# Six short attention tiles: exponentials transposed by TensorE in place of a split, a DMA and a join

## The chip, the cores and the metric

The kernel runs on one core of a Trainium2 chip, in one launch. The metric is the device time of one execution in microseconds (us); lower is better. Engines are named as in the profile: PE is TensorE's matmul, PEld its weight load, DVE is VectorE, ACT is ScalarE, POOL is GpSimd, and SP is the engine that issues most of the DMAs.

## The reference

The input x has 2 batches of 2048 rows of 512 numbers. All arithmetic is in f32.

```python
xn = layernorm(x)
# attention, causal, one head of width 512
x_norm = layernorm(xn) * gamma + beta
q, k, v = (x_norm @ qkv[:, i * 512 : (i + 1) * 512] for i in range(3))
scores = where(causal, q @ k.T / sqrt(512), -inf)
s = softmax(scores) @ v @ o_proj + xn
# mixture of 8 experts, the best two of each row
top, idx = top_k(xn @ gate_w.T + gate_b + bias, 2)
h = silu(xn @ w1[e].T + b1[e]);  y_e = h @ w2[e].T + b2[e]
g = silu(sum of y_e over the two experts, weighted by softmax(top))
return x + s * g
```

Softmax over the keys of a row means: the maximum of its scores, exponentials of the scores less the maximum, their sum as a divisor, and the product of the exponentials with v.

## The kernel before

Rows are taken in tiles of 128. There are 32 tiles, 16 to a batch. The program has three stages. In the first one the rows are normed and projected, and the experts' routing is worked out. In the second one the experts run. In the third one, which starts at about 595 us and is the one that matters here, attention runs and the outputs are put together. The order of instructions on every engine is the order in which the program writes them (a manual schedule), so an engine that waits holds up all that stands behind it.

The attention stage is a loop over steps s. Tiles are taken in the order of `seq`: the first batch from its last tile to its first, so that s = 15 is tile 0, then the second batch in the order 8, 9, 0, 1, 6, 7, 2, 3, 4, 5, 10 to 15. Tile t of a batch sees t + 1 blocks of 128 keys. `widths[s]` holds these keys cut into chunks of at most 512. In step s the program writes, in this order:

- `attended(s - 3)` (ScalarE line 1237, VectorE line 1240) and `emit(s - 4)` (two POOL operations, lines 1248 and 1249, and the output's DMA), for tiles outside the pairs named `FAST`.
- `fetch_inputs(s - 1)`: the DMA of the tile's input rows, on SP.
- `chunk_scores(s, j)` for each chunk (TensorE line 963; on VectorE the mask, line 968, and the maximum, line 969), and in between, on VectorE, `join_p(s - 1, j)` (line 1051).
- `end_scores(s)`: the negated maximum `nm` (VectorE line 981); `divisor(s - 1)`: `ri` (lines 1200 and 1201).
- `exponentials(s)`: for each chunk the exponential on ScalarE (line 1035, into `pr`), a POOL copy that puts the upper and lower 16-bit halves of the f32 numbers apart (line 1039, into `pu`), and a transposing DMA of the 16-bit halves (line 1044, SP, into `puT`).
- `fetch_parts`: DMAs of keys, values and queries for later steps, on SP.
- `values(s - 2)`: the product of the transposed exponentials with v (TensorE line 1069), for tiles outside `FAST`.
- in odd steps `gate(s - 3)` (four VectorE operations, lines 1227 and 1228, and a Silu on ScalarE, line 1232) and `gather_y(s - 1)` (four indirect DMAs on POOL, line 1216).

`join_p` puts the transposed halves together again into `turned[s]`, the tile `pT` that the product takes as stationary operand. A tile's exponentials so pass ScalarE, POOL, a DMA and VectorE, from step s to step s + 1, ahead of their product in step s + 2. `FAST` holds the pairs of tiles with s from 0 to 7 and from 26 to 31, whose product is made with seven half-size products in place of eight (line 1122); the tiles in between, s from 8 to 25, take `values`.

Buffers that matter: PSUM pool `ps_a` with five buffers of 128x512 f32, tag "a", for the scores; `ps_b` with three for the products; `pr` three, `pu` three, `puT` five, `pT` three. ScalarE switches between the table of the exponential and that of Silu with a table load, once each in two steps.

A transpose by TensorE is used elsewhere in the kernel: in `keys(0)` for the first four tiles of rows (line 286, copied from PSUM by ScalarE, line 287), and in `keep_scores` (line 322).

Of the kernel before, what the change touches and what calls it, by code (L numbers as in the profile page):

```python
# [10 lines left out]
F32 = mybir.dt.float32  # L11
# [9 lines left out]
P = 128  # L21
# [5 lines left out]
def gated_attention_moe(  # L27
# [27 lines left out]
    nc = tc.nc  # L55
# [3 lines left out]
    NT = B * S // P  # L59
    BT = 4  # L60
    TB = BT * P
    NB = NT // BT
    NBB = S // TB
# [31 lines left out]
    ident = const.tile([P, P], F32, name="ident")  # L95
# [856 lines left out]
    widths, scored, halves, turned, sums, gates, outs = {}, {}, {}, {}, {}, {}, {}  # L952
# [5 lines left out]
    def chunk_scores(s, j):  # L958
        b, t, first = place(s)
        w = widths[s][j]  # L960
        ps = ps_a.tile([P, TB], F32, name=f"ps_{s}_{j}", tag="a")
        for c in range(ND):
            nc.tensor.matmul(  # L963
                ps[:, :w], lhsT=aqs[seq[s] // 2][:, c, ts(t % 2, P)], rhs=aks[first + j][:, c, :w],
                start=(c == 0), stop=(c == ND - 1),
            )
        if first + j == b:
            nc.vector.tensor_tensor(ps[:, w - P : w], ps[:, w - P : w], keep, ALU.min)
        nc.vector.tensor_reduce(scored[s][0][:, j : j + 1], ps[:, :w], AX.X, ALU.max)  # L969
        scored[s][2].append(ps)  # L970

    def begin_scores(s):
        b, t, first = place(s)
        widths[s] = [TB] * (b - first) + [(t + 1) * P]
        mx = sm.tile([P, NBB], F32, name=f"mx_{s}", tag="mx")
        nm = sm.tile([P, 1], F32, name=f"nm_{s}", tag="nm")
        scored[s] = mx, nm, []
# [13 lines left out]
    ps_a = psum(att, name="ps_a", bufs=5)  # L991
# [13 lines left out]
    for i in range(NS):  # L1005
        experts_step(i)
        if i >= 8 and i % 2 == 0 and early:
            f, b, c = early.pop(0)
# [14 lines left out]
    tp = left(name="tp", bufs=3)  # L1023
# [4 lines left out]
    def exponentials(s):  # L1028

        _, nm, chunks = scored.pop(s)  # L1030
        rs = sm.tile([P, NBB], F32, name=f"rs_{s}", tag="rs")
        sums[s], halves[s] = rs, []
        for j, w in enumerate(widths[s]):
            pr = pp.tile([P, TB], F32, name=f"pr_{s}_{j}", tag="pr")
            nc.scalar.activation(  # L1035
                pr[:, :w], chunks[j][:, :w], AF.Exp, bias=nm, accum_out=rs[:, j : j + 1]
            )
            pu = php.tile([P, 2 * TB], U16, name=f"pu_{s}_{j}", tag="pu")
            nc.gpsimd.tensor_copy(  # L1039
                pu[:, : 2 * w].rearrange("p (h d) -> p h d", h=2),  # L1040
                pr[:, :w].bitcast(U16).rearrange("p (d h) -> p h d", h=2),
            )
            puT = php.tile([P, 2 * BT, P], U16, name=f"puT_{s}_{j}", tag="puT", bufs=5)
            nc.sync.dma_start_transpose(out=puT[:, : 2 * w // P, :], in_=pu[:, : 2 * w])
            halves[s].append(puT)

    def join_p(s, j):
        w = widths[s][j]
        if j == 0:
            turned[s] = tp.tile([P, NBB * TB], F32, name=f"pT_{s}", tag="pT")  # L1050
        nc.vector.tensor_copy(  # L1051
            turned[s][:, j * TB : j * TB + w].bitcast(U16).rearrange("p (i t h) -> p i t h", t=P, h=2),
            halves[s][j][:, : 2 * w // P, :].rearrange("p (h i) t -> p i t h", h=2),
        )

    def values(s):
        po = ps_b.tile([P, D], F32, name=f"po_{s}", tag="b")
        product(po, s, 0, place_keys(s), slice(0, D))
        outs[s] = po

    def place_keys(s):

        return place(s)[1] + 1 + (place(s)[0] - place(s)[2]) * BT

    def product(dst, s, k0, k1, cols, start=True):

        first = place(s)[2]
        for k in range(k0, k1):
            nc.tensor.matmul(  # L1069
                dst, lhsT=turned[s][:, ts(k, P)], rhs=avs[first + k // BT][:, k % BT, cols],  # L1070
                start=(start and k == k0), stop=(k == k1 - 1),
            )
# [9 lines left out]
    def combine_v(b, parts=(1, 2, 3, 4)):  # L1082

        n = 1 if b % NBB == NBB - 1 else 2
        v = avs[b].rearrange("p (i h) d -> p i h d", h=2)[:, :n]
        if 1 in parts:
            avts[b] = cp.tile(
                [P, n, 4, D // 2], F32, name=f"vT_{b}", tag=f"vT{n}", bufs=(1 if n == 1 else NBB - 1)
            )
        t1, t2, t3, t4 = (avts[b][:, :, i, :] for i in range(4))  # L1090
        b11, b12, b21, b22 = (v[:, :, h, c] for h in range(2) for c in (LO, HI))
        for i, dst, x1, x2 in (1, t1, b12, b11), (2, t2, b22, t1), (3, t3, b22, b12), (4, t4, b21, t2):
            if i in parts:
                nc.vector.tensor_tensor(dst, x1, x2, ALU.subtract)
# [109 lines left out]
    def fetch_inputs(s):  # L1204
        n = seq[s]
        xt = op.tile([P, D], F32, name=f"xo_{s}", tag="xo", bufs=5)
        nc.sync.dma_start(out=xt, in_=xb[:, n, :])
        gates[s] = [xt]
# [25 lines left out]
    def attended(s):  # L1234
        n = seq[s]
        o = outs[s] if s // 2 in FAST else op.tile([P, D], F32, name=f"o_{s}", tag="o", bufs=4)
        nc.scalar.activation(  # L1237
            o, outs[s], AF.Identity, scale=sums[s], bias=xshift[:, n : n + 1]
        )
        nc.vector.scalar_tensor_tensor(  # L1240
            o, gates[s][0], xscale[:, n : n + 1], o, ALU.mult, ALU.add
        )
        outs[s] = o

    def emit(s):
        xt, g = gates.pop(s)
        o = outs.pop(s)
        nc.gpsimd.tensor_tensor(o, o, g, ALU.mult)  # L1248
        nc.gpsimd.tensor_tensor(o, o, xt, ALU.add)  # L1249
        nc.sync.dma_start(out=ob[:, seq[s], :], in_=o)  # L1250
# [39 lines left out]
    def fetch_parts(s, most):  # L1290
        while parts_b and most and parts_b[0][0] <= s:
            _, f, b, c = parts_b.pop(0)
            f(b, c)
            most -= 1

    for s in range(NT + OUT + 2):
        fast = s // 2 - 1 in FAST
        if s < NT and s:
            begin_scores(s)
        if s == 1:  # L1300
            fetch_parts(s, 2 * ND)
        for k in range(NT):
            if k not in AHEAD:
                wait = 4 - k % 2 if k // 2 in FAST else 3
                if s == k + wait:
                    attended(k)
                if s == k + wait + 1:
                    emit(k)
        for k in range(NT):
            if s == (NT - 1 if k in AHEAD else k + 2 - k % 2 if k // 2 in FAST else k + 1):  # L1310
                fetch_inputs(k)
        joins = []
        if 0 <= s - 1 < NT - 1:
            joins = [(join_p, s - 1, j) for j in range(len(widths[s - 1]))]
        if s < NT:
            for j in range(len(widths[s])):
                if s:
                    chunk_scores(s, j)
                if joins:
                    f, *args = joins.pop(0)  # L1320
                    f(*args)
                if s == 2 and j:
                    for b in (0, 1) if j == 1 else (j,):
                        combine_v(b, (1,))
        for f, *args in joins:
            f(*args)
        if s < NT and s:
            end_scores(s)
        if fast and s % 2 == 0 and s < NT:
            combine_p(s - 2, range(NBB) if s == 2 else ())  # L1330
        if 0 <= s - 1 < NT:
            divisor(s - 1)
        if s < NT:
            exponentials(s)
            fetch_parts(s, 4 if s else 2 * ND)
            if s in combine:
                combine_v(combine[s])
        if fast and s % 2 == 0:
            values_first(s - 2)

            if s != NT - 2:
                values_next(s - 2)
        elif fast and s == NT - 1:
            values_next(s - 3)
            gate(s - 1)
            values_end(
                s - 3,
                [lambda j=j: join_p(s, j) for j in range(len(widths[s]))] + [lambda: combine_p(s - 1)],
            )
            for k in AHEAD:  # L1350
                make_ahead(k)
        elif fast:
            values_end(s - 3)
        elif 0 <= s - 2 < NT:
            values(s - 2)

        for k in range(0, NT - 2, 2):
            if s == (k + 2 if k + 2 in AHEAD else k + 3):
                gate(k)
        for k in range(0, NT, 2):  # L1360
            if s == (k if k in AHEAD else k + 1):
                gather_y(k)
                gather_y(k + 1)
# [45 lines left out]
```

## Time and profile before

| | us |
|---|---|
| median of 3 runs | 1072.64 (1067.35 to 1072.9) |
| the profiled execution | 1072.68 |
| its span | 1071.0 |
| TensorE busy | 1051.0 (98%) |
| VectorE busy | 598.7 (56%) |
| POOL busy | 422.1 (39%) |
| ScalarE busy | 310.6 (29%) |
| POOL split copies, line 1039, 80 of them | 85.1 |
| VectorE joins, line 1051, 80 of them | 61.0 |
| TensorE products of `values`, line 1069 | 82.9 |

The span is what the profile covers; 1.7 us of the execution's time lie around it. Busy times of the engines lie beside each other, so they don't add up to the span. A line of the profile names the engine, the line of the program, the operation, and output and inputs with buffer numbers left out. A matmul of f32 has two records on TensorE; a transpose of f32 has one. A bracket behind a line of a timeline tells how long the engine sat idle before it, and what is taken to have released it.

### The profile page before, as it was taken

How to read it: one execution, taken by the hardware profiler on the slowest of the kernel's cores; microseconds unless marked ns; L12 is line 12 of the kernel's file. 1: busy time of each engine (PE TensorE's matmuls, PEld its weight loads, DVE VectorE, ACT ScalarE, POOL GpSimd, SP SyncE). 2: the span in 40 equal slices, each digit the busy share in tenths (PEclk: the TensorE clock that was granted, in tenths of full speed). 3: DMA queues.
4: the chain of work that ended last, by engine and by line, in shares of the span. 5: the costliest groups of instructions: out<-in, count | busy, mean ns of one | idle time of the engine just before them, and what ended most of it. 6: DMA issues, size and time to landing. Idle time of an engine off the chain costs nothing.

```text
span 1071.0 us, 12108 instructions
## 1 busy us (share of the span) xinstructions
PE 1051.0 (98%) x3566; PEld 620.9 (58%) x3566; DVE 598.7 (56%) x1181; ACT 310.6 (29%) x659; POOL 422.1 (39%) x463
## 2 busy tenths in 40 slices
PE   8999999999999999999999999999999999999998
PEld 3687886444555555555545446776664444446677
DVE  5797884775333333333345338535555667675756
ACT  3212221211322232322355121312333343332330
POOL 2363240003433333333331023244557677574452
PEclk9999999999999999999999999999999999999999
DMA  8599989936999999999985186355668777763451
GB/s 305 170 282 280 276 257 335 351 123 176 225 222 234 226 227 227 232 226 224 214 187 131 42 224 145 91 122 156 154 176 231 219 201 207 202 171 91 108 141 40
DMA packets 303775, 210.11 MB, mean 196 GB/s; under 512 B 237784, under 2 KB 250840, under 8 KB 302688
## 3 DMA queue, kind: packets, MB, share of 16 engines
q1 hardware_dynamic: 284512, 146.91, 55.1%
q0 software_dynamic: 10560, 35.17, 13.1%
q10 hardware_dynamic: 8640, 27.27, 7.1%
q8 instruction: 30, 0.49, 0.2%
q14 instruction: 33, 0.27, 0.1%
HBM read 92.89 MB, written 60.03 MB: 143 GB/s over the span
## 4 chain that ended last, share of the span: by engine, by line
PE 65%; issue 13%; POOL 8%; DMA 5%; DVE 5%; SPq 2%; ACT 2%; ACTq 0%; POOLq 0%; DVEq 0%
PE ph L879 15%; PE py L918 15%; PE ps L963 13%; PE p L1122 10%; PE p L400 5%; PE pw L207 3%; DMA puT<-pu 2%; PE p L1069 2%; POOL yg L1216 2%; POOL pu L1039 1%; DMA zuT<-zu 1%; POOL o L1249 1%; POOL o L1248 1%; PE po L1069 1%; POOL zu L264 1%
## 5 line engine op out<-in xcount | busy, mean ns | idle before, releaser
L963 PE MATMUL ps<-k,q 128*128 128x512 f32 (+3 forms) x640 | 239.1, 529 | 0.0
L963 PEld LDWEIGHTS ps<-k,q 128*128 128x128 f32 x640 | 117.7, 190 | 122.0 <-issue 112.1
L918 PE MATMUL py<-w,ht 128*128 (+3 forms) x408 | 187.0, 594 | 0.0
L879 PE MATMUL ph<-w,xT 128*128 (+1 forms) x544 | 173.2, 460 | 0.7 <-POOL keep L1001 0.7
L1039 POOL COPY pu<-pr 128x1024 uint16<-128x1024 uint16 (+3 forms) x80 | 85.1, 1092 | 176.1 <-ACT pr L1035 158.1
L926 DVE COPY y<-py 128x512 f32<-128x512 f32 x68 | 46.9, 690 | 177.4 <-PE py L918 177.4
L879 PEld LDWEIGHTS ph<-w,xT 128*128 128x128 f32 (+1 forms) x544 | 97.5, 181 | 74.1 <-issue 35.2
L904 ACT ACTIVATE ht<-ht,b1sel 128x128 f32<-128x128 f32 (+3 forms) x237 | 73.1, 375 | 231.8 <-DVE ht L898 231.8
L889 POOL COPY hu<-h 128x704 uint16<-128x704 uint16 x68 | 52.3, 769 | 206.8 <-ACT h L887 145.5
L918 PEld LDWEIGHTS py<-w,ht 128*128 128x128 f32 (+3 forms) x408 | 73.5, 182 | 75.4 <-issue 37.4
L765 POOL DMA_INDIRECT xs<-zu_d,toki x68 | 69.1, 1017 | 75.7 <-DVE toki L642 64.3
L1035 ACT ACTIVATE pr<-ps,nm 128x512 f32<-128x512 f32 (+3 forms) x80 | 49.1, 621 | 151.3 <-DVE ri L1200 136.1
L1069 PE MATMUL po<-v,pT 128*128 128x512 f32 x182 | 82.9, 603 | 5.8 <-DVE ri L1200 3.3
L969 DVE TENSOR_REDUCE mx<-ps 128x1 f32<-128x512 f32 (+3 forms) x80 | 48.6, 608 | 67.3 <-PE ps L963 66.0
L1216 POOL DMA_INDIRECT yg<-y_d,posi x64 | 66.8, 1044 | 38.4 <-DVE g L1227 21.0
L1051 DVE COPY pT<-puT 128x1024 uint16<-128x1024 uint16 (+3 forms) x80 | 61.0, 770 | 25.6 <-DMA puT<-pu 25.4
L264 POOL COPY zu<-z 128x1024 uint16<-128x1024 uint16 x32 | 35.2, 1100 | 80.3 <-DVE z L249 80.3
L1069 PEld LDWEIGHTS po<-v,pT 128*128 128x128 f32 x182 | 34.7, 194 | 45.8 <-issue 43.0
L413 DVE TENSOR_TENSOR so<-p,so 128x512 f32<-128x512 f32 x70 | 46.0, 686 | 15.7 <-PE p L400 7.4
L1240 DVE SCALAR_TENSOR_TENSOR o<-xo,xscale,o 128x512 f32<-128x512 f32 x30 | 27.4, 925 | 47.2 <-ACT o L1237 39.6
L839 DVE COPY xT<-xhT 128x1024 uint16<-128x1024 uint16 x68 | 46.8, 688 | 12.2 <-DMA xhT<-xs 7.1
L1248 POOL TENSOR_TENSOR o<-o,g 128x512 f32<-128x512 f32 x30 | 40.4, 1348 | 14.7 <-DVE o L1240 14.5
(216 smaller groups left out, 1443.8 us busy)
## 6 DMA issues: line engine op xcount, KB each, us to landing
y_d<-y SPq DMA_DIRECT2D x68, 256.0 KB, 3.7
zu_d<-zu SPq DMA_DIRECT2D x32, 264.0 KB, 5.4
x<-in_x_dram SPq DMA_DIRECT2D x32, 256.0 KB, 4.8
kt_d<-kT ACTq DMA_DIRECT2D x8, 1024.0 KB, 6.0
k<-kt_d SPq DMA_DIRECT2D x32, 256.0 KB, 4.4
q<-qt_d SPq DMA_DIRECT2D x32, 256.0 KB, 3.9
v<-v_d SPq DMA_DIRECT2D x32, 256.0 KB, 5.0
xo<-in_x_dram SPq DMA_DIRECT2D x32, 256.0 KB, 3.8
```

Source lines behind the costliest of these rows:

```text
L400: nc.tensor.matmul(ps[:, r, :], lhsT=lhs[:, c, ts(r, P)], rhs=rhs[:, c, :], start=(c == 0), stop=(c == 1),)
L765: nc.gpsimd.indirect_dma_start(out=xs, out_offset=None, in_=zu_d, in_offset=bass.IndirectOffsetOnAxis(ap=toki[:, i : i + 1], axis=0),)
L879: nc.tensor.matmul(ph[at, :], lhsT=xT[:, c, at], rhs=rhs[k], start=(c == 0), stop=(c == ND - 1),)
L889: nc.gpsimd.tensor_copy(hu[:, :, :H], h.bitcast(U16).rearrange("p (d h) -> p h d", h=2))
L904: nc.scalar.activation(ht[:hn, c, at], ht[:hn, c, at], AF.Silu, bias=b1sel[:hn, c, j : j + 1])
L918: nc.tensor.matmul(py[at, :], lhsT=ht[:k, c, at], rhs=rhs[n], start=(c == 0), stop=(c == NH - 1),)
L963: nc.tensor.matmul(ps[:, :w], lhsT=aqs[seq[s] // 2][:, c, ts(t % 2, P)], rhs=aks[first + j][:, c, :w], start=(c == 0), stop=(c == ND - 1),)
L1039: nc.gpsimd.tensor_copy(pu[:, : 2 * w].rearrange("p (h d) -> p h d", h=2), pr[:, :w].bitcast(U16).rearrange("p (d h) -> p h d", h=2),)
L1051: nc.vector.tensor_copy(turned[s][:, j * TB : j * TB + w].bitcast(U16).rearrange("p (i t h) -> p i t h", t=P, h=2), halves[s][j][:, : 2 * ...
L1069: nc.tensor.matmul(dst, lhsT=turned[s][:, ts(k, P)], rhs=avs[first + k // BT][:, k % BT, cols], start=(start and k == k0), stop=(k == k1 - 1),
L1122: nc.tensor.matmul(dst, lhsT=a[:, k], rhs=v(k), start=(k == 0), stop=(stop and k == n - 1))
L1216: nc.gpsimd.indirect_dma_start(out=y, out_offset=None, in_=y_d, in_offset=bass.IndirectOffsetOnAxis(ap=posi[k][:, n : n + 1], axis=0),)
```

## The change

A tile with at most three blocks of keys takes another path from its exponentials to `pT`. These are s = 13, 14, 15 (3, 2 and 1 blocks) in the first batch and s = 18, 19, 22 (1, 2 and 3 blocks) in the second; each has a single chunk. For them the POOL copy, the transposing DMA and the join on VectorE are left out. In their place `turn_p(s - 1)`, written directly behind `values(s - 2)`, transposes `pr` block by block on TensorE into one PSUM buffer of `ps_a`, and ScalarE copies that buffer into `pT`. The steps with a `turn_p` are s = 14, 15, 16, 19, 20 and 23.

```diff
@@ exponentials(s), behind the exponential of a chunk
+            if by_te(s):
+                halves[s].append(pr)
+                continue
             pu = php.tile([P, 2 * TB], U16, name=f"pu_{s}_{j}", tag="pu")
...
+    def by_te(s):
+
+        return sum(widths[s]) <= 3 * P
+
+    def turn_p(s):
+        n = sum(widths[s])
+        pt = ps_a.tile([P, TB], F32, name=f"pt_{s}", tag="a")
+        for k in range(n // P):
+            nc.tensor.transpose(pt[:, ts(k, P)], halves[s][0][:, ts(k, P)], ident)
+        turned[s] = tp.tile([P, NBB * TB], F32, name=f"pT_{s}", tag="pT")
+        nc.scalar.copy(turned[s][:, :n], pt[:, :n])
@@ the loop over steps
         joins = []
-        if 0 <= s - 1 < NT - 1:
+        if 0 <= s - 1 < NT - 1 and not by_te(s - 1):
             joins = [(join_p, s - 1, j) for j in range(len(widths[s - 1]))]
...
         elif 0 <= s - 2 < NT:
             values(s - 2)
+            if s - 1 < NT and by_te(s - 1):
+                turn_p(s - 1)
```

## The prediction

> **What bounds the kernel now.** I read the page's first part, then the waits of TensorE over the attention stage, then the timelines of the stretch where they fall.
>
> ```profile
> PE 1051.0 (98%) x3566; PEld 620.9 (58%) x3566; DVE 598.7 (56%) x1181; ACT 310.6 (29%) x659; POOL 422.1 (39%) x463
> ```
>
> TensorE is busy for 98% of the span, so the kernel is bound by TensorE nearly everywhere; what can be won is what is left of its idle time, and what it does at a lower clock. The waits of TensorE from 784 us (when the tiles of the first batch run without the seven-product scheme) to 930 us hold two rows; columns are who waited, for whom, total us, times, longest us:
>
> ```profile
> PE po L1069 <- DVE ri L1200: 3.3, 1, 3.3
> PE po L1069 <- DVE pT L1051: 2.5, 3, 1.5
> ```
>
> All four lie ahead of a tile's product with the values. From the widths of the products in the TensorE timeline the tiles can be named (8 matmul records of scores and 2 of values per block; step s does scores(s), then values(s-2)). In these lines: start us, duration us, what, and in brackets the idle time before it.
>
> ```profile
> 823.00 3.60 PE L1069 MATMUL po<-v,pT 128*128 128x512 f32 x8
> 826.43 1.05 PE L963 MATMUL ps<-k,q 128*128 128x128 f32 x8
> 830.80 4.36 PE L1069 MATMUL po<-v,pT 128*128 128x512 f32 x6 [3.32 <-DVE ri L1200]
> 855.48 7.99 PE L1069 MATMUL po<-v,pT 128*128 128x512 f32 x18 [0.49 <-DVE pT L1051]
> 865.71 8.82 PE L1069 MATMUL po<-v,pT 128*128 128x512 f32 x20 [0.51 <-DVE pT L1051]
> 922.39 2.81 PE L1069 MATMUL po<-v,pT 128*128 128x512 f32 x6 [1.46 <-DVE pT L1051]
> ```
>
> So values(12), scores(15), then 3.32 us of nothing, then values(13): a tile with three blocks, one that the change touches. The others wait 0.49 (values(16)), 0.51 (values(17)) and 1.46 us (values(23)); these tiles keep the old path. The long wait costs more than itself. The table of one-us windows shows it (window, its length, busy us of TensorE, its weight loads, VectorE, ScalarE and POOL with counts, then granted clock, DMA share, GB/s):
>
> ```profile
> 829.00:830.00 1.00, 0.00 (x0) 0.00 (x0) 0.89 (x1) 0.00 (x0) 1.00 (x1) 1.00 1.12 379
> 831.00:832.00 1.00, 1.00 (x2) 0.48 (x3) 0.00 (x0) 1.00 (x1) 0.00 (x0) 0.50 0.97 369
> ```
>
> The clock is halved behind the wait and is back at 1.00 by the window from 834 us. values(13) lasts from 830.80 to the next scores at 835.00, 4.20 us, against 2.58 us for six records at full speed (values(12) took 3.43 us for eight). Loss by clock: 1.62 us. Behind the 1.46 us wait the six records took 2.81 us by the merged line, so no clock was lost there.
>
> Why values(13) waits is in the VectorE and ScalarE timelines:
>
> ```profile
> 826.55 0.42 DVE L969 TENSOR_REDUCE mx<-ps 128x1 f32<-128x256 f32 x1
> 829.11 1.54 DVE L1051 COPY pT<-puT 128x768 uint16<-128x768 uint16 x1 [2.14 <-DMA puT<-pu]
> 830.58 0.14 DVE L981 TENSOR_REDUCE nm<-mx 128x1 f32<-128x1 f32 x1
> ```
> ```profile
> 830.79 1.28 ACT L1035 ACT_TABLE_LOAD   x1 [5.33 <-DVE ri L1200]
> ```
>
> join_p(13) at 829.11 stands on VectorE between the maximum of scores(14) and nm(14). It waits for the transposing DMA of tile 13 and ends at 830.65 (the divisor ri, which the wait is put down to, only ended last). So the DMA holds up two things: values(13), and through nm(14) the next exponential (its table load starts at 830.79). That second effect repeats in every step and makes the side engines late.
>
> **What the Trainium skill says.** "TensorE: Matmul & The Clock Gate", Part 1 (the HAM clock gate), says that an idle window of about 3.4 us puts the clock to half and that about 3.4 us of work brings it back; the trace agrees: 3.32 us idle, about 3.3 us at 0.50. The same page, Part 4 (PE-mode transpose), gives about 275 ns for a transpose in a kernel and says that the result lands in PSUM and must be copied out; the trace has 272 to 273 ns per f32 transpose of 128x128. "DMA: Bandwidth & Descriptors", DMA Transpose (X-bar), Constraints, allows 2-byte types only, which is why the old path splits f32 into halves and joins them. "ScalarE: Activation LUTs", Table sets, says that copy is in every set, so the added copies bring no table load; the trace's plain copies between exponentials and products show none.
>
> **The change, part by part.** Touched are tiles with one to three blocks: s = 13, 14, 15 of the first batch (3, 2, 1 blocks) and s = 18, 19, 22 of the second (1, 2, 3), 12 blocks in all, each tile in a single chunk.
>
> *Removed, per tile:* one pu copy on POOL (this shape's means: 128x768 1.04, 128x512 0.75, 128x256 0.54 us, 4.7 us in six), one transposing DMA on SP (about 1.2 us of issue and 2.3 to 5.8 us to landing), one join on VectorE (0.68, 0.91, 0.48 us on average, 4.1 us in six, plus its waits). None of it is TensorE's; its worth is what it lets start earlier.
>
> *Added on TensorE:* 12 transposes. What they take in the stream isn't the record's length, since they overlap:
>
> ```profile
> 66.53 0.60 PE L322 MATMUL pgt<-ident,part 128*128 128x128 f32 x4
> 66.97 1.89 PE L400 MATMUL p<-kT,wqk 128*128 128x256 f32 x8
> ```
>
> Four of this shape and form take 66.97 - 66.53 = 0.44 us, 0.11 us each; 12 take 1.32 us. Upper bound by the record's 0.273 us: 3.3 us. Lower bound: 0, where they fill idle time. I take 0.11.
>
> *Added on ScalarE:* six copies from PSUM, of 3, 2, 1, 1, 2, 3 blocks. The trace has 0.586 us for 128x512 and 0.375 us for 128x256, so about 0.48, 0.375 and 0.27, some 2.3 us in all on an engine that is busy for 29%. Each stands behind exponentials(s) and ahead of the Silu of gate() or the next tile's scaling (line 1237), and waits for values(s-2) and the transposes. The scaling waits for values(s-2) anyway; Silu at an odd step now does too.
>
> *Moved waits, step 14:* join_p(13) is gone from between 826.97 and 830.58, so nm(14) comes at 826.9 instead of 830.58. Table load 827.1 to 828.4, exponential 0.48, then the copy for tile 13 from 828.9 to 829.4; TensorE followed the join by 0.15 us (830.65 to 830.80), so values(13) starts at about 829.5. Meanwhile TensorE does values(12) to 826.43, three transposes to 826.76, scores(15) to 827.81. A wait of 1.7 us stays, now for nm(14), table load, exponential and copy on ScalarE. Start of values(13): 830.80 - 829.5 = 1.3 us earlier, its three transposes included. At 1.7 us idle I expect no fall of the clock (1.46 brought none, 3.32 did): another 1.62 us.
>
> *The later waits.* values(16), (17) and (23) wait for joins whose data left the exponential late. Exponential 16 began at 848.64, because nm(16) came behind a scaling step (842.45) that came behind gate(12), which began at 836.75 behind join_p(14) and nm(15). Replayed without the joins: nm(15) at 831.8, gate(12) 831.9 to 834.5, Silu to 835.7, scaling and VectorE's line 1240 to 837.3 (2 us later if POOL slows it as at 842.45); then nm(16) waits only for scores(16), which end at 840.0: nm(16) 840.9 and exponential 16 from 842.2, 6 us earlier, while TensorE is 3 us earlier. Its joins are ready in time. In the second batch nm(19) no longer waits 2.40 us for join_p(18), nor nm(20) for a join that took 1.98 us, nor nm(23) for 0.47 us: the side engines gain 5 us or more by step 22 against 4 us of TensorE, so I put 0.49 + 0.51 + 1.46 = 2.46 us as won. If they win nothing there, 0.
>
> *Sum against the profiled execution* (1072.68 us, span 1071.0; the median of the runs shown is 1072.64, so the same): 1.3 + 1.62 + 2.46 - 9 further transposes at 0.11 (0.99) = 4.4 us. From 926 us to the last products TensorE has no idle time, so nothing gives it back: 1072.7 - 4.4 = 1068.3 us.
>
> *At nothing:* POOL and SP only lose work; fetch_parts, inputs and outputs behind the removed DMA on SP are issued 1.2 us sooner. pr is held until the transposes instead of until pu: with three buffers the third chunk of exponential 16 needs transposes(15), at about 841.9, and would run at 844; if that cover goes, it costs the difference on ScalarE only. pT of three buffers: tile 10 is long used.
>
> **The rivals.** 0.5% (5.4 us) is about what a measurement of this kernel can tell from no change.
>
> *The whole stall goes.* Without pu(13) beside it, VectorE's gate in step 13 need not take 1.05 us for an instruction of 0.48, so nm(14) may come 0.6 us sooner, and lighter DMA may do more. All idle time lost less 1.32: 3.32 + 1.62 + 2.46 - 1.32 = 6.1, 1066.6 us. For it: DMA engines at a share above 1 around 824 to 831 us. Against: the exponential's table load stays in the chain.
>
> *Little comes of it.* The clock falls anyway (1.62 lost) or the later waits stay (2.46 lost): 1069.9 to 1070.8; both, 1072.4. For it: 1.7 us of wait is above the 1.46 that is known harmless. Against: the replay's slack.
>
> *Slower: the scores' PSUM ring.* ps_a has five buffers and turn_p takes one. The second chunk of scores(17) then needs the bank of the first chunk of exponential 16, where before it was the third chunk. That read ended at 849.3; with TensorE 3 us ahead, the second chunk is due at about 845.3. In my replay the read ends at 842.9 to 844, 1.3 us or more ahead. If ScalarE has not gained (the copies hold Silu, gate is slow), the wait is 4.0 us and the clock falls again, 1.6: 1068.3 + 5.6 = 1073.9 us. It decides from a read that ends later than 845.3, and is a loss against before once it is 2.8 us later than that, with the clock. A like wait at scores(24) or (26) could double it, 1079.
>
> That the path is not taken isn't open: six tiles satisfy the width, in steps where values(s) is called.
>
> **How the numbers follow.** Forecast 45%: 1068.3, from 1067 to 1070. Whole stall goes 25%: 1066.6, to 1065.5 with the scatter of runs (1067.35 to 1072.9 before). Little 17%: 1070 to 1072.4. Ring 13%: 1073.9, half of it worse. Range 1065.5 to 1073.5. Faster than 1067.3 (0.5%): most of the second and a little of the first, 0.30; slower than 1078: half of the last, 0.07; within: 0.63.
>
> **What would show it.** Right: values(13) starts 1 to 2 us after scores(15) at clock 1.00; nm(14) directly behind the maximum of scores(14); the six pu copies and DMAs gone; TensorE's waits for pT in the second batch gone; 12 transposes at about 0.11 us. Wrong: a clock of 0.5 behind 827 us; scores(17) waiting for line 1035; values(14), (15), (18), (19) or (22) waiting for a ScalarE copy; transposes above 0.2 us apart.

## The result and the profile after

| | before | changed |
|---|---|---|
| median of 12 runs, us | 1072.03 (1067.35 to 1075.1) | 1066.09 (1063.41 to 1070.98) |
| profiled execution, us | 1072.68 | 1066.91 |
| its span, us | 1071.0 | 1065.2 |

The ratio of changed to before is 0.9956, with a 95% interval from 0.994 to 0.9971: 0.44% faster. It is worked out from all the runs and is not the quotient of the two medians (0.9945). The page of the changed kernel begins with the engines' busy times:

```profile
PE 1049.3 (99%) x3578; PEld 621.0 (58%) x3578; DVE 595.0 (56%) x1175; ACT 312.1 (29%) x665; POOL 419.1 (39%) x457
```

Against the kernel before, the counts differ by 12 transposes on TensorE, six joins on VectorE, six copies on ScalarE and six split copies on POOL, as the change intends. The lines of TensorE's timeline that answer to those shown of before (start us, duration us, what, idle time ahead of it):

```profile
822.45 3.60 PE L1084 MATMUL po<-v,pT 128*128 128x512 f32 x8
825.88 0.49 PE L1058 MATMUL pt<-ident,pr 128*128 128x128 f32 x3
826.21 1.06 PE L963 MATMUL ps<-k,q 128*128 128x128 f32 x8
828.40 2.84 PE L1084 MATMUL po<-v,pT 128*128 128x512 f32 x6 [1.14 <-ACT pT L1060]
...
851.23 7.89 PE L1084 MATMUL po<-v,pT 128*128 128x512 f32 x18
...
860.68 8.75 PE L1084 MATMUL po<-v,pT 128*128 128x512 f32 x20
...
916.34 3.60 PE L1084 MATMUL po<-v,pT 128*128 128x512 f32 x8
```

values(12), three transposes, scores(15), a wait of 1.14 us in place of 3.32, and values(13). values(16), (17) and (23) wait for nothing. The clock stays at 1.00 behind the wait (window, length, busy us of TensorE, its weight loads, VectorE, ScalarE and POOL, granted clock, DMA share, GB/s):

```profile
827.00:828.00 1.00, 0.26 (x3) 0.07 (x1) 0.00 (x0) 0.99 (x4) 0.92 (x2) 1.00 1.01 374
829.00:830.00 1.00, 1.00 (x4) 0.51 (x3) 0.94 (x1) 0.03 (x1) 0.93 (x1) 1.00 0.47 158
```

VectorE has nm(14) directly behind the maximum of scores(14), and ScalarE goes from there to the copy for tile 13:

```profile
825.43 0.43 DVE L969 TENSOR_REDUCE mx<-ps 128x1 f32<-128x256 f32 x1
825.89 0.15 DVE L981 TENSOR_REDUCE nm<-mx 128x1 f32<-128x1 f32 x1
```
```profile
826.12 1.28 ACT L1035 ACT_TABLE_LOAD   x1 [1.77 <-DVE ri L1215]
827.41 0.47 ACT L1035 ACTIVATE pr<-ps,nm 128x256 f32<-128x256 f32 x1
...
827.88 0.47 ACT L1060 COPY pT<-pt 128x384 f32<-128x384 f32 x1
```

Exponential 16 belongs to a long tile of nine blocks, whose product is values(16). Its first chunk starts at 848.64 us before (first line) and at 842.46 in the changed kernel (second line):

```profile
848.64 0.69 ACT L1035 ACTIVATE pr<-ps,nm 128x512 f32<-128x512 f32 x1
842.46 0.69 ACT L1035 ACTIVATE pr<-ps,nm 128x512 f32<-128x512 f32 x1
```

Profiled executions reach this stretch at different times. scores(13) start at 814.40 us before and at 813.85 in the changed kernel, and between 810.09 and 817.90 over all kernels below, though nothing was changed ahead of them. So the table below counts from the start of scores(13), which takes these differences out. Its first four columns of times are us from one profiled execution each. One execution is not exact either: e2 has no change ahead of scores(18), and yet its exponential 16 starts at 32.9, where before, e4 and e9 have 34.2. A difference of about 1.3 us there, in a single trace, is therefore not clear of scatter. Each ratio is to runs of the kernel before taken together with the runs of its row (their medians are 1071.18 to 1071.31 for the experiments), so medians of different rows compare only roughly.

| kernel | exponential 16 starts | values(16) starts | scores(26) start | end of the span | median of runs | ratio to before (95%) |
|---|---|---|---|---|---|---|
| before | 34.2 | 41.1 | 111.5 | 256.6 | 1072.03 | |
| changed | 28.6 | 37.4 | 105.9 | 251.4 | 1066.09 | 0.9956 (0.994 to 0.9971) |
| e1_first_batch | 28.6 | 37.4 | 106.0 | 251.3 | 1065.28 | 0.9952 (0.9935 to 0.9968) |
| e2_second_batch | 32.9 | 39.7 | 110.1 | 255.4 | 1070.49 | 0.9989 (0.9975 to 1.0003) |
| e3_join_behind_nm | 33.2 | 40.0 | 108.7 | 253.8 | 1069.72 | 0.9985 (0.9972 to 0.9998) |
| e4_fill | 34.2 | 41.3 | 111.3 | 256.4 | 1071.31 | 0.9999 (0.9989 to 1.0009) |
| e9_fill_three | 34.2 | 41.1 | 111.5 | 256.5 | 1072.11 | 1.0016 (1.0002 to 1.003) |
| e10_tile_13 | 32.7 | 39.5 | 109.2 | 254.3 | 1069.79 | 0.9984 (0.9972 to 0.9995) |
| e5_vector_copy | 28.9 | 36.0 | 105.2 | 250.6 | 1066.2 | 0.9949 (0.9929 to 0.9968) |
| e6_four_blocks | 29.0 | 38.4 | 107.4 | 252.4 | 1066.29 | 0.9955 (0.9935 to 0.9975) |
| e7_six_times | 28.9 | 39.3 | 111.1 | 256.6 | 1071.76 | 1.0001 (0.9985 to 1.0017) |
| e8_ahead | 28.7 | 37.0 | 111.9 | 257.3 | 1071.79 | 0.9995 (0.9983 to 1.0007) |
| e11_four_tiles | 28.9 | 36.0 | 104.8 | 250.2 | 1063.48 | 0.9931 (0.9911 to 0.995) |

### The profile page after: what moved, and what is told of

It reads as the page before. It is cut to its first block, busy times and chain, and to the rows that moved or that the text cites. A ratio compares the mean times of both kernels' runs of the same rounds, so it can differ in the third digit from the quotient of the medians.

```text
span 1065.2 us, 12109 instructions
## 1 busy us (share of the span) xinstructions
PE 1049.3 (99%) x3578; PEld 621.0 (58%) x3578; DVE 595.0 (56%) x1175; ACT 312.1 (29%) x665; POOL 419.1 (39%) x457
## 3 DMA queue, kind: packets, MB, share of 16 engines
q0 software_dynamic: 10560, 35.17, 12.6%
## 4 chain that ended last, share of the span: by engine, by line
PE 69%; issue 10%; DMA 6%; POOL 6%; DVE 3%; SPq 3%; ACT 2%; ACTq 0%; POOLq 0%; DVEq 0%
PE ps L963 18%; PE ph L879 15%; PE py L918 15%; PE p L1137 10%; PE po L1084 5%; PE pw L207 3%; DMA zuT<-zu 2%; PE p L1084 2%; POOL zu L264 1%; SPq L271 1%; DMA puT<-pu 1%; POOL pu L1042 1%; SPq L273 1%; POOL yg L1231 1%; DMA zu_d<-zu 1%
## 5 line engine op out<-in xcount | busy, mean ns | idle before, releaser
L1042 POOL COPY pu<-pr 128x1024 uint16<-128x1024 uint16 (+2 forms) x74 | 79.7, 1107 | 170.6 <-ACT pr L1035 145.2
L918 PEld LDWEIGHTS py<-w,ht 128*128 128x128 f32 (+3 forms) x408 | 73.5, 182 | 75.4 <-issue 37.4
L1066 DVE COPY pT<-puT 128x1024 uint16<-128x1024 uint16 (+2 forms) x74 | 55.7, 760 | 17.6 <-DMA puT<-pu 17.5
L1084 PEld LDWEIGHTS po<-v,pT 128*128 128x128 f32 x182 | 34.2, 190 | 39.5 <-issue 36.1
L1263 POOL TENSOR_TENSOR o<-o,g 128x512 f32<-128x512 f32 x30 | 41.3, 1377 | 14.7 <-DVE o L1255 14.5
```

The lines of the kernel that those rows point to most:

```text
L918: nc.tensor.matmul(py[at, :], lhsT=ht[:k, c, at], rhs=rhs[n], start=(c == 0), stop=(c == NH - 1),)
L1042: nc.gpsimd.tensor_copy(pu[:, : 2 * w].rearrange("p (h d) -> p h d", h=2), pr[:, :w].bitcast(U16).rearrange("p (d h) -> p h d", h=2),)
L1066: nc.vector.tensor_copy(turned[s][:, j * TB : j * TB + w].bitcast(U16).rearrange("p (i t h) -> p i t h", t=P, h=2), halves[s][j][:, : 2 * ...
L1084: nc.tensor.matmul(dst, lhsT=turned[s][:, ts(k, P)], rhs=avs[first + k // BT][:, k % BT, cols], start=(start and k == k0), stop=(k == k1 - 1),
```

## The experiments

**Which tiles.**

```diff
 def by_te(s):
-    return sum(widths[s]) <= 3 * P
+    return s < NT // 2 and sum(widths[s]) <= 3 * P     # e1_first_batch
+    return s >= NT // 2 and sum(widths[s]) <= 3 * P    # e2_second_batch
+    return s == 13                                     # e10_tile_13
```

> The changed kernel with the new path for tiles 13, 14 and 15 only (6 of the 12 blocks). Theory (waits): what is won is the wait ahead of values(13) with its half clock, and the lateness that the joins of these three tiles put on the maxima behind them. Then values(13) waits about 1.1 us at clock 1.00, values(16) and values(17) wait for nothing, and only the wait of values(23), 1.5 us, may stay: 4 to 5.5 us less than before. Rival (relief): the gain is in proportion to the work taken from POOL, SP and the DMA engines: half the blocks, half the gain, about 2.8 us.

Measured: 0.9952, the whole gain with half the blocks. TensorE in this kernel waits 1.13 us ahead of values(13), then not until values(23):

```profile
825.24 2.84 PE L1084 MATMUL po<-v,pT 128*128 128x512 f32 x6 [1.13 <-ACT pT L1060]
...
913.22 3.67 PE L1084 MATMUL po<-v,pT 128*128 128x512 f32 x8 [0.55 <-DVE pT L1066]
```

The rival that puts the gain in proportion to the work taken from POOL, SP and the DMA engines is out: the 2.8 us that it expects would be a ratio of 0.9974, outside the interval (0.9935 to 0.9968). The second batch's tiles only take the 0.55 us wait, and pay for it with six transposes.

> The changed kernel with the new path for tiles 18, 19 and 22 only. Theory (waits): the 3.3 us wait of values(13) and the half clock stay, values(16) and values(17) still wait about 0.5 us each, values(23) no longer waits: 1.6 us less for that wait, 0.7 us more for six transposes, so about 1 us less than before. Rival (relief): about 2.8 us less, as in the first batch.

Measured: 0.9989, about 1.2 us. The interval (0.9975 to 1.0003) does not tell it from no gain; the trace's end is also 1.2 us sooner. That is what the theory of waits said, but it did not come in the way it said. In this execution join_p(13) ended sooner than before without any change there, and values(13) waited 1.99 us and kept its clock; then values(16) waited 2.04 us and lost the clock instead:

```profile
827.01 2.81 PE L1084 MATMUL po<-v,pT 128*128 128x512 f32 x6 [1.99 <-DVE ri L1215]
851.68 9.69 PE L1084 MATMUL po<-v,pT 128*128 128x512 f32 x18 [2.04 <-DVE pT L1066]
```

values(16) takes 7.89 us at full clock. What TensorE won at the first wait it paid at the second; e9 and e10 below go into this.

> The changed kernel with the new path for tile 13 alone (3 of 12 blocks). Theory (waits): the start of values(13) and its clock are won as in the changed kernel; join_p(14) and join_p(15) are back ahead of nm(15) and nm(16), so exponential 16 is later than in the changed kernel, and values(16), (17) and (23) may wait 0.5 to 1.5 us each: 2.5 to 4.5 us less than before. Rival (relief in proportion to the blocks): a quarter of the gain, 1.4 us.

Measured: 0.9984, or 1.7 us (interval 0.5 to 3.0). That is near the rival's 1.4 us, and the theory's lower end of 2.5 lies in the interval too, so the time alone decides nothing; the trace shows what happened. values(13) starts 14.5 us behind scores(13), the same as in the changed kernel (before: 16.4). But join_p(14) is back on VectorE (first fence), where it waits 3.67 us for its DMA ahead of nm(15), and values(16) waits 2.26 us (second fence) and takes 9.66 us where it takes 7.89 at full clock:

```profile
831.64 0.43 DVE L1066 COPY pT<-puT 128x512 uint16<-128x512 uint16 x1 [3.67 <-DMA puT<-pu]
831.99 0.15 DVE L981 TENSOR_REDUCE nm<-mx 128x1 f32<-128x1 f32 x1
```
```profile
851.02 9.66 PE L1084 MATMUL po<-v,pT 128*128 128x512 f32 x18 [2.26 <-DVE pT L1066]
```

**The clock alone.** The kernel before, with unused matmuls where TensorE sat idle:

```diff
         elif 0 <= s - 2 < NT:
+            if s == 15:
+                idle = ps_b.tile([P, D], F32, name="idle", tag="b")
+                for _ in range(7):          # e4_fill; 3 in e9_fill_three
+                    nc.tensor.matmul(
+                        idle, lhsT=turned[s - 3][:, :P], rhs=avs[0][:, 0, :], start=True, stop=True
+                    )
             values(s - 2)
```

> The kernel before, with seven unused f32 matmuls of 128x512 (3.0 us) written ahead of values(13), where TensorE sat idle for 3.3 us. Theory (the half clock comes from the idle time): the clock stays at 1.00 and values(13) takes 2.6 us in place of 4.2; at the most 1.6 us less than before, less still if the side engines are the ones that are late. Rival (the clock falls for another reason): still 0.50 for about 3.3 us, and the time is the same or longer.

Measured: the same time, 0.9999. My 3.0 us was half of what seven such matmuls take: 6.01 us, since each has two records of 0.43. They ran 2.7 us past the join's end at 829.2, and all of that cost nothing:

```profile
825.89 6.17 PE L1358 MATMUL idle<-v,pT 128*128 128x512 f32 x14
831.90 2.74 PE L1069 MATMUL po<-v,pT 128*128 128x512 f32 x6
```

The clock did what the theory said: values(13) took 2.58 us, and the mean clock was 0.999 or 1.000 in 15 of 20 runs, where the kernel before had that in 1 of 51.

> The kernel before with three unused f32 matmuls of 128x512 ahead of values(13), 2.6 us by the 0.86 us each that seven took in the run before (6.0 us in all). Theory (the half clock of the kernel before comes from this one wait, in nearly all of its runs): values(13) starts when its join is done, as before, the mean clock rises to 0.999 or 1.000, and 1.5 to 2 us are won. Rival (the lost clock comes back elsewhere, or does not set the end): mean clock as before, or no gain.

Measured: 1.0016 (1.0002 to 1.003), no gain, so the rival holds in its second form: the lost clock did not set the end. values(13) ran at full clock and scores(16) began 19.0 us behind scores(13), 1.6 us sooner than before. Then values(16) waited 2.05 us where it had waited 0.49, and over the runs the mean clock was 0.999 or more in only 4 of 14:

```profile
829.95 2.81 PE L1069 MATMUL po<-v,pT 128*128 128x512 f32 x6 [0.73 <-DVE ri L1200]
854.63 7.99 PE L1069 MATMUL po<-v,pT 128*128 128x512 f32 x18 [2.05 <-DVE pT L1051]
```

Before, e4 and e9 start exponential 16 at 34.2 us, whatever TensorE does. So in these three the time of values(16), and with it of all behind it, is set by VectorE and ScalarE to within 0.2 us (41.1, 41.3 and 41.1), not by TensorE's waits ahead of it.

**The join's place on VectorE.** The kernel before, with the joins of the six tiles moved behind the exponentials of the next tile:

```diff
+        late = bool(joins) and sum(widths[s - 1]) <= 3 * P
+        if not late:
             for f, *args in joins:
                 f(*args)
         ...
             exponentials(s)
+            if late:
+                for f, *args in joins:
+                    f(*args)
```

(Inside the loop of chunks the joins of these tiles are left out as well.)

> The kernel before, with join_p of the six tiles moved on VectorE behind the maximum, nm, the divisor and the exponentials of the next tile; no transposes by TensorE. Theory (the join holds up nm): exponential 14 comes 3 to 4 us earlier; values(13) still waits for its own join, 2.5 to 3.3 us, and the clock still falls; the waits of values(16), (17) and (23) go or shrink: 1.5 to 3 us less than before. Rival (relief): no work is taken from POOL, SP or the DMA, so nothing is gained, and the waits stay.

Measured: 0.9985, 1.6 us (interval 0.2 to 3.0), at the low end; the trace's end is 2.8 us sooner. nm(14) came behind its maximum, 12.6 us behind scores(13) (before: 16.2; changed: 12.0), but the DMA wait went from nm to gate(12), which now stood behind join_p(14):

```profile
830.51 0.15 DVE L981 TENSOR_REDUCE nm<-mx 128x1 f32<-128x1 f32 x1
...
839.64 0.43 DVE L1051 COPY pT<-puT 128x512 uint16<-128x512 uint16 x1 [3.49 <-DMA puT<-pu]
839.98 0.48 DVE L1227 TENSOR_SCALAR g<-yg,share 128x512 f32<-128x512 f32 x1
```

Exponential 16 gained only 1.0 us, which is within the scatter that e2 shows. values(23) no longer waited, which agrees with the theory; values(16) and (17) still did (0.98 and 0.51 us), which does not. The wait of values(13) was 3.31 us, as long as before, and its clock stayed at 1.00. That is this one execution: over the 22 runs the mean clock was 0.9976, against 0.9975 in the 51 runs of the kernel before.

**The transposes' price.**

```diff
-        for k in range(n // P):
+        for k in [k for k in range(n // P) for _ in range(6)]:
             nc.tensor.transpose(pt[:, ts(k, P)], halves[s][0][:, ts(k, P)], ident)
```

> The changed kernel with each transpose made six times into the same place: 60 transposes more. Theory (0.11 us each in the stream): 6.6 us more than the changed kernel, less about 1.1 us that fills the wait ahead of values(13): 5.5 to 6.6 us more, so about as slow as before. Rival (each costs its record of 0.27 us): 16 us more.

Measured: scores(26) 5.2 us later than in the changed kernel. With the 1.14 us wait that the transposes fill, 60 of them take 6.3 us, 0.105 each. In one group, twelve take from 829.72 to 831.03, 0.109 each:

```profile
829.72 1.47 PE L1058 MATMUL pt<-ident,pr 128*128 128x128 f32 x12
831.03 2.31 PE L963 MATMUL ps<-k,q 128*128 128x512 f32 x5
```

The record's 0.27 us is out as a price.

**The place of turn_p and of its copy.** For e8_ahead the call was moved ahead of `exponentials(s)`:

```diff
+        if 0 <= s - 1 < NT and by_te(s - 1):
+            turn_p(s - 1)
         if s < NT:
             exponentials(s)
 ...
             values(s - 2)
-            if s - 1 < NT and by_te(s - 1):
-                turn_p(s - 1)
```

> The changed kernel with turn_p(s - 1) written ahead of exponentials(s), so its transposes stand ahead of values(s - 2) on TensorE and its copy ahead of the exponential on ScalarE. Theory: values(13) no longer waits (1.1 us less), but TensorE now waits ahead of transposes for exponentials that are not done: for exponential 14 about 0.6 us, for exponential 18 about 2 us, and for others where the side engines are late: 1 to 4 us more than the changed kernel. Rival (the place behind the values does not matter): 1 us less than the changed kernel.

Measured: as slow as before (0.9995); scores(26) 6 us later than in the changed kernel, more than expected. The wait ahead of values(13) is gone, and TensorE waits for exponentials instead, three times (who, for whom, total us, times, longest):

```profile
PE pt L1058 <- ACT pr L1035: 5.0, 3, 2.4
```

Waits of 0.6 and 2 us were foreseen for tiles 14 and 18, and were 0.79 and 2.38; 1.85 us at tile 22 was not named, nor was it foreseen that the clock would fall behind the 2.38 (values(17) took 10.18 us up to the next scores, where it takes 8.59 at full clock).

```diff
-        nc.scalar.copy(turned[s][:, :n], pt[:, :n])
+        nc.vector.tensor_copy(turned[s][:, :n], pt[:, :n])   # e5_vector_copy
```

> The changed kernel with turn_p's copy on VectorE in place of ScalarE, so that it no longer stands behind the table load and the exponential. Theory: the 1.1 us that is left of the wait ahead of values(13) is ScalarE's queue; on VectorE the copy runs right behind the divisor at about 826.3 us, and that wait goes: about 1 us less than the changed kernel, 6 to 7 us less than before. Rival: the copy now holds up gate() on VectorE at odd steps, Silu and the scaling come later, and a new wait of some other product gives the 1 us back.

Measured: 0.9949. In the trace values(13) waits for nothing, and scores(26) start 0.8 us sooner than in the changed kernel, as the theory said; a wait of 0.37 us appears at values(17). The copy on VectorE stands right behind the divisor:

```profile
824.66 0.16 DVE L1216 RECIPROCAL ri<-ri 128x1 f32<-128x1 f32 x1
824.92 0.56 DVE L1060 COPY pT<-pt 128x384 f32<-128x384 f32 x1
```

The ratios (0.9949 and 0.9956, with overlapping intervals) don't tell the two kernels apart.

```diff
-        return sum(widths[s]) <= 3 * P
+        return sum(widths[s]) <= 4 * P    # e6_four_blocks
```

> The changed kernel with the new path for tiles of up to four blocks: tiles 12 and 23 too (8 blocks more). Theory: no wait of those two tiles is left to take away, so it costs their 8 transposes, 0.9 us, less what an earlier nm(13) (it stood behind the DMA wait of join_p(12)) takes from the 1.1 us wait of values(13): between 1 us less and 1 us more than the changed kernel. Rival (relief: what counts is the work taken from POOL, SP and DMA): two thirds as much again as the first 12 blocks brought, some 3.5 us less.

Measured: 0.9955, no gain on the changed kernel; scores(26) 1.5 us later by the trace, a little more than expected. 0.9 us are the eight transposes; the wait ahead of values(13) grew from 1.14 to 1.72 us. ScalarE's timeline shows why: the copy for tile 12 waits until values(11) and the transposes behind it are done, and Silu of gate(10) stands behind the copy:

```profile
817.60 0.58 ACT L1060 COPY pT<-pt 128x512 f32<-128x512 f32 x1 [2.88 <-PE po L1084]
818.20 1.28 ACT L1247 ACT_TABLE_LOAD   x1
819.49 1.06 ACT L1247 ACTIVATE g<-g 128x1024 f32<-128x1024 f32 x1
```

The scaling behind Silu comes later, and nm(14) is 13.1 us behind scores(13) in place of 12.0.

**A version from what was found.** Tiles 13, 14, 15 and 22, with the copy on VectorE:

```diff
-        return sum(widths[s]) <= 3 * P
+        return s in (13, 14, 15, 22)
...
-        nc.scalar.copy(turned[s][:, :n], pt[:, :n])
+        nc.vector.tensor_copy(turned[s][:, :n], pt[:, :n])
```

> The changed kernel with the new path for tiles 13, 14, 15 and 22 only, and its copies on VectorE. Theory: tiles 18 and 19 had no wait to take away, so their three transposes (0.3 us) are saved; the copy on VectorE takes the last 1.1 us of wait ahead of values(13); tile 22 keeps values(23) free of its 0.5 us wait: about 1 us less than the changed kernel, 6 us or a little more less than before. Rival: joins of tiles 18 and 19 are what keeps the second batch late, and waits of 0.5 to 1.5 us come back at values(20) to values(23).

Measured: 0.9931 (0.9911 to 0.995) over six runs, the fastest of all; its interval overlaps that of the changed kernel, while the trace has scores(26) 1.1 us sooner than there, as expected. Tiles and copy were changed at once; against e5, which has the same copy and all six tiles, scores(26) are 0.3 us sooner, which is what three transposes take. From 780 us to the end only short waits are left on TensorE, the longest of them

```profile
PE po L1084 <- DVE pT L1066: 0.4, 1, 0.4
```

## Why the prediction was right, and where it was not

The forecast was 1068.3 us, from 1065.5 to 1073.5; the median is 1066.09. The direction held, and so did the chain from join_p(13) through nm(14) to values(13) and exponential 16. The size was in the range: the ratio gives 4.7 us and the medians 5.9, where 4.4 was forecast and 6.1 in the second case. From scores(13) to scores(26) the two traces differ by 111.50 - 105.92 = 5.6 us where the sum said 4.4; over the rest 0.3 us was given back, for which I found no single wait. The other 0.55 us of the spans' difference lies ahead of scores(13).

- *Start of values(13), 1.3 us.* It was 16.4 - 14.55 = 1.85. The chain on ScalarE was as predicted, and the start of it was 0.55 us earlier: without pu(13) beside it, the VectorE operation of gate(10) took 0.48 us instead of 1.05. The five traces with pu(13) all have 1.04 or 1.05 there, the eight without it all 0.48. The prediction had this effect under its second case, with 0.6 us.
- *The clock, 1.62 us.* It was 4.20 - 2.68 = 1.52: values(13) took 2.68 us up to the transposes, against 4.20. Over the 12 runs of the changed kernel the mean clock was 0.9992, against 0.9975 over the 51 of before beside e1; by these means an estimated 0.9 and 2.7 us were lost out of 1068, a difference of 1.8.
- *The later waits, 2.46 us.* All three went, and together they gave 3.2 us. Each took a little more with it than its own length: from scores(19) to values(17) it was 2.40 us before and 1.72 changed, 0.68 for a wait of 0.51. With the 1.85 and 1.52 and less the transposes this makes the 5.6 us. The prediction laid part of it to the joins of the second batch. By e1, values(16) and (17) are freed by the first batch's tiles alone, and so is most of the wait of values(23); the second batch's tiles take only its last 0.55 us.
- *Nine further transposes, 0.99 us.* Right: 0.105 to 0.11 us each, by e7 and by the trace.
- *Ring of PSUM buffers.* It didn't bind. Exponential 16 began at 842.46 and ended its first chunk at 843.15; the second chunk of scores(17) was due near 844.3, 1.2 us later, close to the 1.3 us that the prediction named.

What did not hold is the form of the sum. It added the start of values(13), the clock and the later waits as if each stood by itself. e9 won 1.6 us at values(13) and lost it at values(16). e10 had the whole of values(13) and kept 2.3 us by its trace. In the changed kernel exponential 16 comes early as well (28.6 in place of 34.2 us), and values(16) starts 3.7 us sooner. Taking the join of tile 13 alone off VectorE gives 1.5 us of that, little more than the scatter; taking off those of tiles 13, 14 and 15 gives 5.6. Tiles 13 and 14 without 15 were not tried. The prediction had worked out that time (exponential 16 "6 us earlier"). So the sum came out because both sides moved, and not because its terms can be had one by one.

Two readings of the prediction were wrong. The eight records of scores are per chunk of keys, not per block, which changes no term. And the DMA's hold on the exponentials does not repeat in every step: before, join_p(14) waited for nothing, since VectorE came late to it.

```profile
835.77 0.75 DVE L1051 COPY pT<-puT 128x512 uint16<-128x512 uint16 x1
```

Where VectorE came to it early, in e10, the same join waited 3.67 us. The wait had been hidden, and taking away the one ahead of it brought it out.

The theory that the gain goes by the work taken from POOL, SP and the DMA engines in proportion is refuted by e1 and e6. That the joins hold up VectorE and ScalarE only through nm is not what e3 shows: moved behind nm, a join holds up the gate in the same way. The traces point to the wait for the DMA in VectorE's queue as what has to go. No run shows that by itself: wherever the join is left out, the split on POOL and the DMA are left out too. By the traces, nm(14) comes 4.1 us sooner; 3.6 of them are the join's wait and length between the maximum and nm (826.97 to 830.58 before), and 0.57 are the faster gate(10), which may come from a lighter POOL. Further on, the two parts were not separated.

Open: the 0.3 us given back behind scores(26), and why profiled executions reach scores(13) at times 7.8 us apart. A part of the spread is one wait of TensorE for a VectorE join at about 92 us, in code that no kernel changes. It was 0.30 us in the earliest (e6) and 3.70 in the latest (e3), and in e3 and before (2.29 us) the clock then fell to a mean of 0.83 from 90 to 100 us, about 1.7 us lost. Wait and clock make up 5.1 of the 7.8 us. Why this wait varies is not known.

## What to carry to other kernels

A wait of the busiest engine may be worth its length only if the engines that feed the next wait get earlier too, as here: fill it or remove it alone, and see whether the next one grows by the same amount. An operation that waits for a DMA in an in-order queue can cost more through what stands behind it than through its own result, and moving it back one place may only change its victim. A join that shows no wait may have one that is hidden by another. Single traces can differ by 1 us in a stretch whose code is the same, so compare several before trusting such a difference. Price a short added operation by the distance of starts in a group of its kind, not by its record.

## What the runs showed of the hardware that was not expected

The clock's fall isn't told by the length of one wait. In the traces it fell behind waits of TensorE of 3.70 us (e3, at about 92 us), 3.32 and 2.29 (before), 2.38 (e8), 2.26 (e10) and 2.04 (e2). It stayed at 1.00 behind, among others, 3.31 us (e3), 2.65 and 2.05 (e9), 2.52 (e5) and 1.99 (e2). So waits of the same length, 3.32 and 3.31 or 2.04 and 2.05, went both ways. No fall was seen behind a shorter wait than 2.04 in these traces. The line shows the wait of 2.65 us in e9; the clock was 1.00 from 90 to 100 us.

```profile
92.89 1.06 PE L307 MATMUL pg<-zT,gw 128*32 128x512 f32 x8 [2.65 <-DVE zT L290]
```

The prediction took 1.46 as safe and 3.32 as fatal and put the line between them; the fall behind 2.29 us stood in the trace of the kernel before as well, ahead of the stretch that it looked at. The Trainium skill, "TensorE: Matmul & The Clock Gate", Part 1, says that the window in which activity is watched is free-running, so its place against a wait differs from run to run. That the same wait went both ways agrees with this. The page also gives about 3.4 us for an idle window that brings the fall, and here falls came behind shorter waits, down to 2.04 us; the measurement decides. Why is open.
